# A two-layer graph attention kernel: the minimum of a merge's elu moved from VectorE to ScalarE, and new places for the steps of a hand-ordered schedule

## The chip, the cores and the metric

The kernel runs on one core of a Trainium2 chip. The metric is the time of one execution on the device in microseconds. A measurement of it is the median of several executions. A separate profiled execution gives the trace: every instruction with its engine, start and end. Its engines are called PE (TensorE's matmuls), PEld (its weight loads), DVE (VectorE), ACT (ScalarE), POOL (GpSimd) and SP (the queue that issues most DMAs).

## What is computed

Sixteen graphs of 1024 nodes with 256 features go through two layers. Layer 0 holds an MLP, an attention without a mask over all nodes ("dense"), a second MLP, and a masked attention; layer 1 is one more masked attention. Cut to what matters:

```python
h = relu(layernorm(x))                       # layer 0
out = relu(h @ mlp1_w + b1); residual = out  # 1024 x 512
out = gat(out, None, W_fc, a_fc)             # dense attention, ends in elu
out = elu(out) + residual                    # the merge: elu of an elu
out = relu(out @ mlp2_w + b2); residual = out
out = gat(out, adj, W_hand, a_hand)          # masked attention "a"
x = x + relu(elu(out) + residual)
h = relu(layernorm(x))                       # layer 1
x = x + relu(masked_gat(h, adj, W, a))       # masked attention "b"
```

with gat: h = inp @ W; e = leaky_relu(f1_i + f2_j); softmax over j; elu(att @ h). All of it is fp32.

## The kernel before

**Stages.** For each graph the dense attention needs no 1024 x 1024 matrix. Since leaky_relu has two branches, each node's mean over all others splits at a threshold into a sum over the nodes below it and a sum over those above. So the rows are ranked (`rank`, L911 ff.), scattered into sorted order in DRAM by GpSimd (`scatter`, L933), read back (`read_sorted`, L977), summed from both sides (`sum_before` L1005/L1007, `sum_behind` L1018/L1020), written as a fine table (L1012) with a coarse table of carried sums (`carry`, L1029 to L1034), and each node gathers its two rows (`gather`, L1044: first "fine", then "coarse" added onto it). `share` (L1056 to L1059) and `mean` (L1065, L1068) make the node's mean out of the gathered row. The first half of graph 0 takes matmuls instead (L1088, L1096). The projection ahead of it is a seven-product scheme for 2 x 2 blocks (`step`, L827, which adds to accumulators that ScalarE copies out in between, L849).

**The merge**, which the change edits, stands for one half h (512 nodes) and one chunk c (128 of 512 features): four transposes on TensorE into a PSUM tile (L1114), the minimum with 0 (L1116), exp (L1117), exp(. - 1) (L1118), which is the elu of the elu but for a constant folded into the later biases. `merge_end` adds max(ps, 0) on VectorE (L1124) and adds the sum to the residual on GpSimd (L1125). After four merges of a half, `mlp2` (L1132, evicted at L1135) reads it. The transposes' PSUM tile stays taken until `merge_end`; there are two such tiles ("tr"), four for matmul results ("mm"), and one double one ("bc").

**Masked attention** (Masked, Gnn0 for "a", Gnn1 for "b"): `project` (L662, L664), `extremes` (L669, L670), `vectors` (a transpose of the maxima at L539, then small VectorE and ScalarE steps, L679 to L691), `send` (a transpose at L544 and a DMA to DRAM) and `row` (a broadcast read back, L700), `scale` (L709), `weight` (L715, VectorE), `product` (L725, TensorE), and `finish`, `combine`, `add` and `update` (L737 to L771).

**Order.** The program is written step by step in the order of a table. `at(name, lo, hi, steps)` (L519 ff.) gives each step a time and adds a hand-set offset:

```python
when = lo + (hi - lo) * i / len(steps) + (moved[k] if k < len(moved) else 0.0)
table.append((when, len(table), step))
```

where `moved` is the entry of the dictionary SHIFT for the key part + name; part is "start ", "first ", "mid " or "end ". All steps are then sorted by `when` (L1532) and emitted; each engine carries out its instructions in that order, GpSimd too, whose order is tied by added dependences. The times have no effect but the order. The calls of `at` put the steps of graph b around base_of(b), with a period of 142 table units; steps of three graphs interleave: masked attention of b, dense attention of b+1, projection of b+2. Four of these calls:

```python
at("masked_first1", t0 + 1, t0 + 1, [m.vectors])
at("masked_first2", t0 + 3.4, t0 + 3.4, [m.send])
at("merges1", lo, lo + 9.2, each(d.merge, [h], range(HC)))
at("merges2", lo + 2.5, lo + 11.7, each(d.merge_end, [h], range(HC)))
```

Of the kernel before, what the change touches and what calls it, by code (L numbers as in the profile page):

```python
# [12 lines left out]
AF = mybir.ActivationFunctionType  # L13
# [18 lines left out]
    "end dense_begin1": (-4.8,),  # L32
    "end dense_begin2": (-4.19, -2.9,),
    "end dense_begin3": (-6,),
    "end dense_begin4": (0, -7.8, -7.7, -9.2, -13.5, -16, -18, -21.5,),
    "end dense_begin5": (-13, -8.9,),
    "end dense_begin6": (-15.56, -15.6, -23.8, -21.56, -18.8, -23.7,),
    "end dense_begin7": (-26.7,),
    "end dense_end1": (-11, -4.4,),
    "end dense_end2": (-10.8, -11.2, -9.8, -3.5, -3.4, 0, -3.1, -3.4,),  # L40
    "end dense_rows1": (-2.2, -2.09, -36.8, -18.9, -45.6, -25, -15.1, -10.1, 0, -24.9, -37.9,
        -13.5, -41.1, -31.4, -13.1, -24.8,),
    "end dense_rows2": (-13.8, -8, 0, 7, -11.8, -10, -21.5, -18.1, -13.6, -12, -13.5, 0, 4.5, 3.7,
        -16.8, -22.8, -10.4, -22.9, -9, -16.2,),
    "end dense_rows3": (0, -2.1,),
    "end dense_rows4": (-15.1,),
    "end dense_sums1": (-54.3,),
    "end dense_sums10": (-40.1,),
    "end dense_sums12": (-5.4,),
    "end dense_sums2": (0, -7.8, 7.9, 0, -6.2, -18.4, -20.7, -21.1,),  # L50
    "end dense_sums3": (-9.4, -4,),
    "end dense_sums4": (-9.7, -10.7, -8.6, -4.2, -4, -1.6, -2.3, -1.1,),
    "end dense_sums7": (-2.5, -3.7, -4.7, -4.3, -4.1, -4.8, -3.8, -4.43,),
    "end dense_sums9": (-2.3,),
    "end early_gathers1": (0, 0.002,),
    "end early_gathers2": (-6.42, -6.4,),
    "end early_gathers3": (12.5, 15.4, 9.3, 14,),
    "end early_gathers4": (0, -1.4, -3.64, 0, 8.4, 7.6, 3.7, 5.7,),
    "end first_mlp1": (-16.5, -17.2, -17.3, -3.7,),
    "end first_mlp2": (-54.3, -50.1, -81.4, -59.3,),  # L60
    "end masked_first1": (-15.6,),
    "end masked_first10": (-10.2, -10.6, -11.3, -10.4, -7, -7.4, -4.4, -5,),
    "end masked_first11": (-10.7, -11.3, -12.3, -9.9, -7.7, -7.4, -5.58, -6.198,),
    "end masked_first12": (-2.91,),
    "end masked_first13": (-12.5, -12.6, -12.6, -11.8,),
    "end masked_first14": (-9.41, -9.3, -12.4, -11.79, 2, 0.7, 0, -0.22,),
    "end masked_first15": (-11.7,),
    "end masked_first16": (-0.4,),
    "end masked_first2": (-15.1,),
    "end masked_first3": (-14.3,),  # L70
    "end masked_first4": (-13.9,),
    "end masked_first5": (-14.5, -14.5, -14.2, -10.7, -12.3, -13.74, -11.2, -12.8,),
    "end masked_first6": (-40.9,),
    "end masked_first7": (-24.2, 0, -18.5, -23.2,),
    "end masked_first8": (0, 0, 10.9, 2.8,),
    "end masked_first9": (-8, -8.5, -9.2, -9.1, -9.9, -8, -8.85, -9.6, -8.1, -7.8, -8.673, -9.54,
        -10.4, -11, -11.4, -11.3, -12.1, -12.7, -12.2, -11.3, -5.5, -4.5, -5.3, -6.16, -7.09, -4.2,
        -4.3, -3.7, -3.7, -4, -3.6, -3.9, -20.3, -12.1, -8.5, -7.3, -6.7, -6.9, -5.8, -5.1,),
    "end masked_second1": (-2.5, -3.1, -3.4, -3.71, -4.3, -4.9, -3.3, -3.3, -3.3, -3.3, -3.3, -3.3,
        -2.4, -2.4, -2.4, -2.4, -2.4, -2.4, -3.9, -2, -2.4, -2.8, 1.4, 1.4, 0, 0.9, 0.5, 0.7, 0.9,  # L80
        0.7, -24.9, -20.7, -20.7, -19.7, -14.1, -6.9,),
    "end masked_second2": (-5.2, -5.2, -1.8, -2.5, -2.1, -2.1, 2.1, 1.7, 0.3, -0.1, -10.9,),
    "end masked_second3": (-5.6, -5.7, -3.1, -2.3, -2.61, 1.2, 1.2, 0.002,),
    "end masked_second4": (-5.5, -3.8, 0, 3.4, -0.4, 0.5, 1.7, 15,),
    "end masked_second5": (40.4, 35, 28.4, 30.2, 28.1, 19.5,),
    "end masked_second6": (23.3, 19.2,),
    "end merges1": (-4.7, -6.7, -5.81, -8.1, 0, -2.6, 3.6, -1.7,),
    "end merges2": (-4.8, -6.5, -5.09, -7.39, 1.7, -0.62, 2.8,),
    "end scatters1": (0, -10.8, -13, -6.9, -16.54, -19.4, -20.05, -27.7,),
    "end second_mlp1": (-4.7, 1, -2.8, -3.8,),  # L90
    "end second_mlp2": (-22.5, -15.6, -13.3, -19.56, -20.4, -16.7, -19.3, -23.1,),
    "end second_mlp3": (-14.7,),
    "end second_norm1": (-6.7, -2.63, -6.7, -8.8, -5.2, -6.1, -7, -7.87,),
    "end second_norm2": (-8.5,),
    "end second_norm3": (-7.9,),
    "end second_norm4": (-8.6,),
    "end second_norm5": (-8.8, -8, -5.9, -8.1, -3.8, -4.4, -6.3, -6.3,),
    "end second_norm6": (-12.1,),
    "end second_norm7": (-14.9,),
    "end turn_at1": (-11.8, -11.8, -11.8, -11.8, -1.2, -1.6, -2, -2,),  # L100
    "end turn_at2": (-9.84, -9.8, -9.84, -9.8, -1.8, -1.8, -1.8, -1.8,),
    "end weights a": (-15.398, -15.1, -15.3, -15.8, -6.2, -14, -7.1, -18.2, -9.2, -11.5, -7.4,
        -18.7, -13.1, -9.4, -7.5, -9.2, -9, -12.2, -9, -8.3, -12.1, -8, -10.2, -14, -8.8, -7.3,
        -8.2, -5.93, -8, -5.9, -6.6, -5.4, -15.5, -12.8, -12.7, -13.6, -15.3, -8.1, -7.7, -7,),
    "end weights b": (-8.4, -8.8, -8.2, -8.6, -9.7, -6.8, -4.6, -2, -7.6, -4.6, -7, -4.6, -1.8,
        -3.2, -1.4, -1.9, -4.9, -5.7, -8.6, -2.4, -5.6, 0, 0, 0, 0, 0, 0, -1.3, 0, 0, -8.8, 0,
        -1.6, 3.34, 0, 0, 0, 2.1, 2.5, 1.5, -22.7, -21.8, -23.1, -42.3, -15.4, -19.8, -11.1,
        -11.9,),
    "first dense_begin1": (-2.9,),
    "first dense_begin2": (0, 0.002,),  # L110
    "first dense_begin3": (-3.39,),
    "first dense_begin4": (3.7, 1.7, 0, -2.6, -4.5, -8.8, -14.1, -13.2,),
    "first dense_begin5": (-6.2, -6.2,),
    "first dense_begin6": (-19, -21, -26.9, -36.497, -21.9, -18.1,),
    "first dense_end1": (-7.5,),
    "first dense_end2": (-6.1, -5, -3.64, -5.2, 8.6, 4.9, 9.2, 3.9,),
    "first dense_rows1": (-16.9, -16.5, -16.7, -16.797, -15.6, -15.6, -17.9, 3.8, 0, 2.5, -29.3,
        -25, -23.9, -19.68, -8.7, -20.8,),
    "first dense_rows2": (-20.8, -20.6, -17.1, -14.6, -18.7, -13.1, -13.4, -12.6, -12.9, -15.1,
        -11.7, 2.03, 0, 3.2, -20.3, -17.5, -10.4, -19.3, -8.4, -7.1,),  # L120
    "first dense_rows3": (-6.5, -1.9,),
    "first dense_rows4": (-11.5,),
    "first first_mlp1": (-7.1, 0, 0, 17.6,),
    "first first_mlp2": (-6.2, -4, -22.9, -6.4,),
    "first first_norm3": (-32.1, -26.6, -29.2, -30, -31.1, -29.4, -21.9, -22.7,),
    "first first_norm4": (-24.9,),
    "first first_norm5": (-36.6, -36.6, -36.6, -36.6, -28, -47.3, -48.1, -27.4,),
    "first first_norm6": (-33.7, -33.7, -33.7, -33.7, -32.7, -34.1, -27.5, -33.4,),
    "first first_norm7": (0, 0.003, 0.003, 0.003,),
    "first gathers1": (4.6, 4.6, 4.6, 4.6, -5.6, 0, 11.4, 11.5,),  # L130
    "first gathers2": (12.8, 13.4, 10.5, 9.9, -9.8, 0, 0, -1.2,),
    "first masked_first1": (-8.2,),
    "first masked_first10": (-6.3, -6.7, -7.6, -7.9, -2.21, -2.3, -4.9, -5.46,),
    "first masked_first11": (-5.8, -7.2, -3.8, -4.6, -2, -2.2, -4.6, -5.19,),
    "first masked_first13": (-9.1, -4.5, -4.7, -8.3, -4.9, -5.6, -7.9, -8.5,),
    "first masked_first14": (-5.1, 0, -3.1, -3.9, -3.2, -4.7, -7.84, -8.44,),
    "first masked_first15": (-6.1,),
    "first masked_first16": (-8.9,),
    "first masked_first4": (-10.2,),
    "first masked_first5": (-7.4, -7.4, -7.4, -7.4, -7.4, -7.4, -7.4, -7.4,),  # L140
    "first masked_first6": (-185.7,),
    "first masked_first8": (4.4, 14.6, 16.2,),
    "first masked_first9": (-5.9, -6.7, -7.1, -7.7, -8.4, -6.6, -7.4, -7.5, -11.7, -9.7, -10.5,
        -9.8, -10, -10.2, -10.6, -8.5, -2.6, -2.6, -2.6, -2.6, -2.6, -2.6, -2.6, -2.6, -4.6, -4.6,
        -4.6, -4.6, -4.6, -4.6, -4.6, -4.6,),
    "first masked_second1": (-31.7, -26.8, -20.2, -18.5, -14.3, -13.7, -4.9, -3.5, -3.7, -2.7, 0,
        0, -6.2, -5.8, -5.2, 0, 0, 0, -1.6, -1.6, -1.6, -1.6, -1.6, -1.6,),
    "first masked_second2": (-13.8, -13.8, 0, 0, 0.8, 0.8, -1.8, -1.8,),
# [164 lines left out]
def fast_path(ctx: ExitStack, tc: tile.TileContext, alarm, x, adj, w1, b1, w2, b2, w_fc, a_fc,  # L313
# [21 lines left out]
    nc = tc.nc  # L335
# [441 lines left out]
    class Dense:  # L777
# [331 lines left out]
        def merge(self, h, c):  # L1109

            ps = tr_psum(f"hpT_{self.b}_{h}_{c}")
# [350 lines left out]
    e = dense[1]  # L1462
# [528 lines left out]
```

## Time and profile before

| what | us |
|---|---|
| median of 3 runs | 2241.82 (2232.39 to 2243.66) |
| the profiled execution | 2232.1 |
| its span, first to last instruction | 2230.4 |
| TensorE busy in it | 2172.5 |
| VectorE, ScalarE, GpSimd busy | 1776.0, 1261.9, 1067.5 |
| granted TensorE clock, mean | 0.997 |

A row of the groups reads: line, engine, operation, out<-in, shapes, count, then the busy time in us and the mean ns of one, then the engine's idle time just before these instructions and what ended it. A row of the waits reads: the waiting engine and line, who ended the wait, the sum in us, how many, the longest. In a row of the timeline the bracket holds the idle time ahead of the instruction and its releaser.

### The profile page before, as it was taken

The numbers are of one execution on the slowest core, as the hardware profiler recorded it, in microseconds if no ns is written. First come the engines' busy times: TensorE is split into PE (matmuls) and PEld (weight loads), VectorE is DVE, ScalarE is ACT, GpSimd is POOL, SyncE is SP. The second block draws the span as 40 slices with busy tenths as digits, with TensorE's granted clock in tenths as the row PEclk, the third lists the DMA queues.
The fourth block names the chain that finished last, engine by engine and source line by source line (L and its number), as shares of the span: only waits on it lengthen the run. The fifth ranks groups of instructions, "written<-read, shape, count | busy, mean of one in ns | idle before, by whom it ended". The sixth has DMA issues, their size and how long they took to land. (4 is left out here: it accounts for less than half of the span.)

```text
span 2230.4 us, 31158 instructions
## 1 busy us (share of the span) xinstructions
PE 2172.5 (97%) x9498; PEld 1672.8 (75%) x9498; DVE 1776.0 (80%) x4929; ACT 1261.9 (57%) x2797; POOL 1067.5 (48%) x1344
## 2 busy tenths in 40 slices
PE   7989999999999999999999999999999999999998
PEld 4757778687876878778687877868788687777777
DVE  7877887788877779887888878778887878869756
ACT  5446655647465573756547465563755657455453
POOL 3343527365362744627375363735537265463520
PEclk9999999999999999999999999999999999999999
DMA  6367758566576756757666575856748574565610
GB/s 226 115 166 202 152 181 189 176 172 173 165 178 191 180 159 187 181 161 173 202 170 166 174 177 178 189 176 178 175 150 202 187 177 136 167 172 161 162 41 28
DMA packets 268751, 373.42 MB, mean 167 GB/s; under 512 B 124880, under 2 KB 180760, under 8 KB 264480
## 3 DMA queue, kind: packets, MB, share of 16 engines
q1 hardware_dynamic: 221968, 207.19, 32.6%
q0 software_dynamic: 45952, 163.99, 28.9%
q8 instruction: 78, 1.28, 0.3%
q14 instruction: 97, 0.79, 0.1%
q10 hardware_dynamic: 656, 0.17, 0.0%
HBM read 231.09 MB, written 126.56 MB: 160 GB/s over the span
## 5 line engine op out<-in xcount | busy, mean ns | idle before, releaser
L725 PE MATMUL ob<-hmb,attb 128*128 128x257 f32 x2048 | 473.3, 381 | 0.4 <-DVE attb L715 0.2
L725 PE MATMUL oa<-hma,atta 128*128 128x258 f32 x2048 | 459.8, 382 | 6.0 <-ACT resT L801 4.4
L725 PEld LDWEIGHTS oa<-hma,atta 128*128 128x128 f32 x2048 | 385.8, 190 | 74.0 <-ACT resT L801 9.2
L725 PEld LDWEIGHTS ob<-hmb,attb 128*128 128x128 f32 x2048 | 382.0, 191 | 57.5 <-issue 5.4
L715 DVE SCALAR_TENSOR_TENSOR atta<-rowsa,qwda,edge 128x256 f32<-128x256 f32 (+1 forms) x520 | 239.8, 494 | 71.8 <-DMA rowsa<-row_a 67.6
L753 POOL TENSOR_TENSOR posa<-posa,onat 128x256 f32<-128x256 f32 x118 | 98.5, 835 | 384.3 <-ACT posa L741 383.6
L715 DVE SCALAR_TENSOR_TENSOR attb<-rowsb,qwdb,edge 128x256 f32<-128x256 f32 (+1 forms) x536 | 268.0, 528 | 8.2 <-PE ob L725 4.1
L1044 POOL DMA_INDIRECT got<-coarse,k x124 | 202.8, 1635 | 96.6 <-DMA got<-fine,k 38.4
L798 PE MATMUL m<-hT,w_sb 128*128 128x512 f32 x512 | 238.4, 596 | 0.3 <-ACT hT L588 0.2
L1132 PE MATMUL m<-resT,w_sb 128*128 128x512 f32 x512 | 229.3, 599 | 8.7 <-POOL resT L1125 8.5
L1125 POOL TENSOR_TENSOR resT<-resT,e 128x512 f32<-128x512 f32 x128 | 167.5, 1320 | 110.6 <-DVE e L1124 103.5
L933 POOL DMA_INDIRECT sorted<-hnat,place x128 | 126.8, 991 | 143.0 <-DVE place L926 53.5
L740 ACT ACTIVATE ea<-oa,reca 128x256 f32<-128x256 f32 x128 | 60.7, 474 | 236.2 <-DVE reca L737 214.1
L1132 PEld LDWEIGHTS m<-resT,w_sb 128*128 128x128 f32 x512 | 95.6, 192 | 118.4 <-issue 99.0
L801 ACT ACTIVATE resT<-m,b_sb 128x512 f32<-128x512 f32 x128 | 87.4, 685 | 159.8 <-PE m L798 159.8
L1044 POOL DMA_INDIRECT got<-fine,k x124 | 130.3, 1051 | 64.7 <-DMA fine<-xs 26.3
L798 PEld LDWEIGHTS m<-hT,w_sb 128*128 128x128 f32 x512 | 96.1, 191 | 80.1 <-issue 73.2
L956 ACT ACTIVATE junk<-r,fs 128x1024 int8<-128x1024 f32 x124 | 142.1, 1146 | 11.1 <-POOL fs L860 6.5
L754 POOL TENSOR_TENSOR ea<-ea,posa 128x256 f32<-128x256 f32 x118 | 99.1, 839 | 90.4 <-ACT ea L747 59.5
L767 ACT ACTIVATE rb<-ob,recb 128x256 f32<-128x256 f32 x128 | 57.9, 474 | 146.0 <-DVE recb L765 136.2
L1068 DVE SCALAR_TENSOR_TENSOR hp<-got,den,part 128x513 f32<-128x513 f32 x120 | 103.9, 878 | 38.6 <-ACT part L1065 36.9
L1117 ACT ACTIVATE e<-e 128x512 f32<-128x512 f32 x128 | 79.9, 624 | 95.7 <-DVE e L1116 94.5
(211 smaller groups left out, 4314.0 us busy)
## 6 DMA issues: line engine op xcount, KB each, us to landing
xs<-sorted SPq DMA_DIRECT2D x32, 1028.0 KB
fine<-tt SPq DMA_DIRECT2D x32, 1026.0 KB
fine<-xs SPq DMA_DIRECT2D x32, 1026.0 KB
x<-in_x_dram SPq DMA_DIRECT2D x16, 1024.0 KB
xn<-in_x_dram SPq DMA_DIRECT2D x15, 1024.0 KB
out_dram<-x SPq DMA_DIRECT2D x28, 512.0 KB
hT<-xn SPq DMA_DIRECT2D x416, 32.0 KB
coarse<-carry SPq DMA_DIRECT2D x32, 256.5 KB
```

What stands on the lines that cost most here:

```text
L715: nc.vector.scalar_tensor_tensor(a_t[:, :n * P], self.rows[:, i], self.qwd[:, 1, j:j + 1], edge[:, j, i], op0=OP.max, op1=OP.mult)
L725: nc.tensor.matmul(self.out[t][:, :F + self.ONES], lhsT=self.att[t0, j][:, (t - t0) * P:(t - t0 + 1) * P], rhs=self.hm[:, j, 2:2 + F + sel ...
L753: adder.tensor_add(pos, pos, o_nat[:, t, :])
L754: adder.tensor_add(e, e, pos)
L798: nc.tensor.matmul(ps, lhsT=w1_sb[:, kc, c * P:(c + 1) * P], rhs=piece(kc, h), start=(kc == 0), stop=(kc == FC - 1))
L801: nc.scalar.activation(self.resT[:, c, h * HALF:(h + 1) * HALF], ps, AF.Relu, bias=b1_sb[:, c:c + 1])
L933: made = nc.gpsimd.indirect_dma_start(out=sorted_d[self.b % 2], out_offset=bass.IndirectOffsetOnAxis(ap=self.place[:, t:t + 1], axis=0), i ...
L956: nc.scalar.activation(junk, self.r2, AF.Sign, bias=self.fs[:, 0, t:t + 1], accum_out=self.signs[:, t:t + 1])
L1044: nc.gpsimd.indirect_dma_start(out=got[u // n][:, u % n, :], out_offset=None, in_=(coarse_d if coarse else fine_d)[self.b % 2][:, :], in_o ...
L1068: nc.vector.scalar_tensor_tensor(hp, got[:, K:], den[:, 0, u:u + 1], part, op0=OP.mult, op1=OP.add)
L1125: nc.gpsimd.tensor_add(dst, dst, e)
L1132: nc.tensor.matmul(ps, lhsT=w2_sb[:, kc, c * P:(c + 1) * P], rhs=self.resT[:, kc, h * HALF:(h + 1) * HALF], start=(kc == 0), stop=(kc == H ...
```

## The change

In `merge` the minimum with 0 leaves VectorE: ScalarE computes relu(-mean) from PSUM, and the first exp takes the scale -1. exp(-relu(-m)) is exp(min(m, 0)), so the result is the same. Beside that nearly all entries of SHIFT get new values, so that nearly every step of the program may stand at another place of the order. The steps themselves are the same 7005 in both.

```diff
             e = work.tile([P, HALF], F32, tag="e2", name=f"e_{self.b}_{h}_{c}", bufs=3)
-            nc.vector.tensor_scalar_min(e, ps, 0.0)
-            nc.scalar.activation(e, e, AF.Exp)
+            nc.scalar.activation(e, ps, AF.Relu, scale=-1.0)
+            nc.scalar.activation(e, e, AF.Exp, scale=-1.0)
             nc.scalar.activation(e, e, AF.Exp, bias=neg1)
```

Of SHIFT, the entries that bear on the steps named below (the diff has some 270 lines more of this kind):

```diff
-    "end early_gathers4": (0, -1.4, -3.64, 0, 8.4, 7.6, 3.7, 5.7,),
+    "end early_gathers4": (-8.55, -6.9, -1.7, -3.7, 9.2, 11.4, 4.7, 4.7,),
...
-    "end dense_end1": (-11, -4.4,),
+    "end dense_end1": (-12.1, -3.3,),
...
-    "mid dense_sums3": (-4.26,),
+    "mid dense_sums3": (-0.158609, -2.5,),
...
-    "mid masked_first1": (-9.2,),
+    "mid masked_first1": (-13.3,),
...
-    "mid masked_first2": (-9.61,),
+    "mid masked_first2": (-12.2,),
...
-    "mid merges1": (1.1, 0, 3.22, 0.92, 7.4, 10.3, 8.1, 5.8,),
-    "mid merges2": (3.6, 1.4, 3.4, 0.5, 5.5, 7.83, 10.4, 9.1,),
+    "mid merges1": (2.75, -2.3, 5, 3.5, 6.8, 4.5, 7.2, 6.6,),
+    "mid merges2": (6.3, 0, 4.5, 2.4, 4.5, 4.1, 7.5, 5.6,),
...
-    "mid second_norm8": (0, -20.95, -9.6, -17.3, -21.9, -14.21, -21.2, -13,),
-    "mid second_norm9": (-4.6,),
+    "mid second_norm8": (-18.9, -20.8, -18.8, -26, -24.9, -25.4, -25.5,),
+    "mid second_norm9": (-16.7,),
...
-    "start merges1": (-14.1, -15.5, -17, -15.4, 0, 5.5, 5, -11.3,),
-    "start merges2": (-16.4, -14.7, -9.8, -9.53, 3.55, 5.6, 3.9, -3.5,),
+    "start merges1": (-20.6, -21.8, -22.6, -24.5, 0, 2.7, 0.43, -10.4,),
+    "start merges2": (-16.4, -16.5, -17.6, -19.4, 7.8, 5.5, 4.8,),
```

In the order that follows, the steps of the middle repeat from period to period, before and after.

## The prediction

> **What bounds the kernel now.** I read the page's head first, then TensorE's share by stretches of the span, then who ended TensorE's waits, and only then the rows of the instructions that the change touches.
>
> ```profile
> span 2230.4 us, 31158 instructions
> ...
> PE 2172.5 (97%) x9498; PEld 1672.8 (75%) x9498; DVE 1776.0 (80%) x4929; ACT 1261.9 (57%) x2797; POOL 1067.5 (48%) x1344
> ```
>
> ```profile
> 0.00:200.00 200.00, 172.27 (x747) 121.25 (x748) 157.58 (x466) 93.85 (x182) 68.56 (x110) 0.97 0.59 174
> 200.00:1960.00 1760.00, 1746.06 (x7593) 1348.09 (x7593) 1426.24 (x3920) 1030.29 (x2308) 902.14 (x1121) 1.00 0.66 175
> 1960.00:2230.40 270.40, 254.14 (x1160) 203.49 (x1159) 192.19 (x543) 137.77 (x309) 96.82 (x114) 0.99 0.40 110
> ```
>
> The columns of the second view are the stretch, its length, then the busy time of PE, PEld, DVE, ACT and POOL, TensorE's granted clock, the DMA share and GB/s. TensorE (PE) is the bound. It is idle 27.7 us in the first 200 us, 13.9 us in the middle 1760 us, and 16.3 us in the last 270 us. The change leaves every matmul as it is, so no more than these 57.9 us (2.6%), and what a stall costs inside the "busy" time, can be won. The waits:
>
> ```profile
> PE m L1132 <- POOL resT L1125: 8.5, 3, 3.9
> ...
> PE oa L725 <- ACT resT L801: 4.4, 7, 1.3
> PE extpsb L539 <- DVE extb L670: 4.0, 2, 3.6
> PE linea_ps L544 <- ACT qwda L687: 3.5, 10, 0.4
> ```
>
> 8.5 us lie in the start (three waits of mlp2 for the merged rows of graph 0), 4.0 in the end, 3.5 are ten waits of one kind, one per period of the middle. The rest are scattered waits of a few tenths, and 10 us before the first transpose.
>
> **The elu's minimum.** Durations from the rows (busy, then mean ns):
>
> ```profile
> L1118 ACT ACTIVATE e<-e,neg 128x512 f32<-128x512 f32 x128 | 92.4, 722 | 4.2
> ...
> L1116 DVE TENSOR_SCALAR e<-hpT 128x512 f32<-128x512 f32 x128 | 84.8, 680 | 10.7 <-PE hpT L1114 10.2 <-issue 0.2
> L1117 ACT ACTIVATE e<-e 128x512 f32<-128x512 f32 x128 | 79.9, 624 | 95.7 <-DVE e L1116 94.5
> ...
> L588 ACT ACTIVATE hT<-nt 128x512 f32<-128x512 f32 x76 | 41.0, 592 | 72.1 <-PE nt L584 72.0
> ```
>
> Removed: 128 VectorE minima by 0.680 us, 87 us of 1776. Added: 128 ScalarE Relus from PSUM. The trace has no such Relu with scale -1, but L588 is a Relu of the same shape from PSUM without a pointer operand: 0.592 us; L801, with a bias pointer, takes 0.685. I take 0.592, 76 us, ScalarE then at 60%; the other end is 88 us. The Exp with scale -1 costs what it cost. Table loads: none, since Relu (L740) and Exp (L746) alternate already and the trace has one table load of 1283 ns in all.
>
> A rule of the Trainium skill speaks against this step: "ScalarE: Activation LUTs", section "Rules for kernel authors", wants relu, max and min on VectorE, which it calls up to about 3x faster per element in bf16. By the rule the minimum would be 0.592/3 = 0.2 us on VectorE, and the change would give up 25 us there for 76 us on ScalarE. By the rows VectorE needs 0.680 on this fp32 PSUM source and ScalarE 0.592, so 87 us are freed for 76. The rows decide. The chain of one merge becomes 0.592+0.624+0.722 = 1.94 us instead of 2.03, but all of it on ScalarE, whose own part was 1.35. So merges that come back to back now leave at one per 1.94 us.
>
> In the middle the merges are not back to back. In table order, counting TensorE's own work between steps (0.217 us per matmul record of 257 columns, 0.109 per transpose, 0.43 per 512 columns), the first half's four merges of a period are spread over 10.1 us instead of 5.6, the second half's over 6.7 instead of 7.6. Between the last merge of the first half and the mlp2 that reads it there are 8.2 us instead of 11.4. Needed: 1.94+0.69 (L1124)+1.32 (L1125) = 3.95 us plus ScalarE's lag. That covers a lag of 4 us. If the cover is gone, TensorE stands for the excess in each period; this is the second rival below. Likeliest: nothing.
>
> **The new places, middle.** The ten waits of the row transpose (L544):
>
> ```profile
> 960.31 0.27 PE L539 MATMUL extpsa<-ident,exta 128*128 128x128 f32 x1
> 960.42 1.03 PE L725 MATMUL ob<-hmb,attb 128*128 128x257 f32 x4
> 961.80 0.27 PE L544 MATMUL linea_ps<-ident,qwda 128*8 128x128 f32 x1 [0.35 <-ACT qwda L687]
> ```
>
> From the transpose of the maxima to the row transpose the chain VectorE, then Exp on ScalarE takes 1.49 us, and one product step (0.87) lies between. The table puts the two at 1.0-9.2 = -8.2 and 3.4-9.61 = -6.21 before, and at -12.3 and -8.8 after; in the new order two product steps (1.74 us) lie between. 1.74 + 0.11 exceeds 1.49, so this wait goes: -3.5 us. What is late next there is the product's wait for mlp1's eviction (L725 <- L801, 4.4 us): its TensorE order (mlp1 c=3, natural 1 and 2, then ga product) is the same after, so 0. VectorE and ScalarE steps are moved throughout; VectorE's 87 us less can only help its queue, ScalarE's 76 more can hurt evictions; bounds -8 to +27 (second rival), taken 0.
>
> **The end.** The longest single wait:
>
> ```profile
> 2092.14 0.45 PE L539 MATMUL extpsb<-ident,extb 128*128 128x128 f32 x1 [3.62 <-DVE extb L670]
> 2092.38 3.46 PE L725 MATMUL ob<-hmb,attb 128*128 128x257 f32 x8
> ```
>
> Eight matmuls in 3.46 us are 0.43 each, twice the usual 0.217: the stretch from 2092 to 2096 shows a granted clock of 0.57, so 1.7 of these 4.0 us are lost too. The chain of work that ended last tells the cause: VectorE stood 6.38 us at the share (L1056) of graph 15's first half until its last coarse gather, issued at 2080.77, landed 10.02 us later, and extb (L669, L670) is queued behind it. "end early_gathers4" moves the first two of these gathers by -8.55 and -6.9: the last is issued 8.9 us of TensorE work ahead of the share instead of 5.2. 3.7 us more cover removes the 3.6 us: -3.6-1.7 = -5.3. On GpSimd's queue the last two coarse gathers (1.64 each) and one fine gather (1.05) now stand ahead of the second root of graph 14's norm (L569, L570: 0.52+1.09), which VectorE's centering just before the share waits for. That is 3.3+1.05+1.6 = 6.0 us of queue from 8.7 us of TensorE work away: covered by 2.7 us; with the cover gone, the excess is TensorE's again, as its turns and the share come behind the centering. I take 0 for it, and -2 to -5.3 for the whole.
>
> **The start.** Before, merge (0,0) begins at 134.58 and the fourth quarter of the first mlp2 at 153.17, with half the clock from 148 to 154. After, TensorE's work ahead of merge (0,0) grows from 111.9 to 116.2 us (dense products and one step are drawn ahead), so it begins near 138.9, and the four merges are paced by ScalarE: 0.4+4x1.94+0.69+1.32 = 10.2, so 149.1. That is 4 us earlier than 153.17. But GpSimd, in order, has coarse gathers of 1.6 us between the adds, and the second half hangs on the landing of its last gather as before. I take -2, between -6 and +8 (back to back merges that end later than reckoned, at half clock).
>
> **Landings.** The profiled execution took 2232.1, its span 2230.4; the median of the three runs is 2241.8, 9.7 above. I take the difference to be landings that came later and what waits for them; no trace here shows a slower execution. The new order gives the sorted rows 9.5 us of TensorE work from read to first use instead of 3.9, and the row of the second layer 10.4 instead of 6.5. It takes back between 0 and 9.7; for want of a row I take 3.
>
> Sum: -3.5-5.3-2-3 = -13.8, from 2241.8 to 2228.0 us, or 2221 for an execution like the profiled one.
>
> **The rivals.** (1) More is won: the new places also clear the scattered waits. The middle's other 10 us, half of the start's 17.8 us beside the first 9.9, and the 9.7 of landings instead of 3 would make another 20: 2208. For it: VectorE is at 80% and waits 67.6 us for row reads. Against: these waits are many and of 0.2 to 0.8 us, each with its own cause. (2) Slower: ScalarE is late in the merges. Its load there now:
>
> ```profile
> 901.40:909.70 8.30, 8.30 (x40) 7.23 (x39) 5.84 (x19) 8.09 (x20) 4.22 (x4) 1.00 0.97 199
> 909.70:918.00 8.30, 8.30 (x45) 7.20 (x44) 6.77 (x17) 6.94 (x18) 7.03 (x8) 1.00 1.00 167
> 918.00:926.20 8.20, 8.20 (x43) 7.11 (x42) 6.58 (x14) 6.83 (x17) 4.86 (x5) 1.00 0.30 61
> ```
>
> The fourth busy column sums to 21.9 of 24.8 us. Eight Relus add 4.7: 26.6, 1.8 too many. ScalarE also evicts the seven-product's accumulators (L849), which TensorE adds to again a few steps later, and mm has four banks; so a lag of over about 4 us is TensorE's wait. 1.8 us in each of 15 batches are 27: 2269. It decides if less than 1.8 us of other ScalarE work leaves this stretch. In the new order four of eight scale steps (L709, 4x0.5 = 2.0 us) leave, but two sign steps (1.3 each) come in at its end. (3) The stalls only move: what is cleared at one place returns at the next queue, 2241.
>
> **How the numbers follow.** Likeliest case 0.42 at 2228 (by itself 2218 to 2238), more won 0.18, stalls move 0.19, slower 0.21. Within 0.5% of 2241.8 is 2230.6 to 2253.0; half a per cent is about what a measurement of this kernel can tell from no change. Of the likeliest case two thirds lie under 2230.6: faster 0.28+0.18 = 0.46; same 0.14+0.19 = 0.33; slower 0.21. The range goes from 2206 to 2258: from the case of more won to the lower part of the slower one.
>
> **What would show it.** Right: no waits of linea_ps on qwda; TensorE's gap before extpsb near the end under 1 us with full clock after it; DVE busy near 1690, ACT near 1338, the new Relu near 0.59; the middle's TensorE idle time near 10 us. Wrong: new waits of TensorE on ScalarE's L849, L664 or L801 between merges, or on L1125, of over 1 us per period; or a start whose mlp2 begins later than 150.

## The result, and the profile after

| | before | after |
|---|---|---|
| median, us (four runs each) | 2240.64 (2232.39 to 2243.66) | 2210.82 (2207.67 to 2213.08) |
| profiled execution / its span | 2232.1 / 2230.4 | 2209.0 / 2207.3 |
| ratio after/before, 95% interval | | 0.9872 [0.9841, 0.9902] |

The change makes the kernel faster by 29.8 us between the medians and by 23.1 us between the two profiled spans. The forecast had the sign, and its range (2206 to 2258) holds the time; but its likeliest case was 2228, and the time is near the first rival's 2208. So more was won than its steps account for.

The head of the page after, with the busy time of each engine:

```profile
PE 2162.5 (98%) x9498; PEld 1678.0 (76%) x9498; DVE 1689.1 (77%) x4801; ACT 1336.2 (61%) x2925; POOL 1064.5 (48%) x1344
```

VectorE (DVE) lost 128 instructions and 86.9 us, ScalarE (ACT) got 128 and 74.3 us. The number of matmuls is the same. The three stretches of the span after, with the columns of the prediction's second view (the third is shorter because the kernel ends earlier):

```profile
0.00:200.00 200.00, 174.72 (x748) 126.12 (x749) 156.43 (x457) 100.44 (x193) 69.87 (x110) 0.95 0.61 177
200.00:1960.00 1760.00, 1755.41 (x7695) 1367.56 (x7694) 1358.05 (x3846) 1104.54 (x2447) 913.05 (x1134) 1.00 0.67 178
1960.00:2207.00 247.00, 232.38 (x1058) 184.29 (x1056) 174.60 (x500) 131.25 (x286) 81.61 (x101) 0.99 0.36 103
```

The count in the second row is the first thing to see: in the same 1760 us TensorE gets through 7695 matmul records instead of 7593. It is idle 4.6 us there instead of 13.9. TensorE's waits over the whole span after, the first four rows (who ended the wait; sum, number, longest, in us):

```profile
PE nt L591 <- DVE hn L581: 11.5, 2, 9.9
PE hpT L1121 <- DVE e L1131: 7.6, 5, 4.1
PE hpT L1121 <- issue: 2.3, 2, 1.9
PE m L805 <- ACT rb L774: 2.2, 6, 0.5
```

(Line numbers after are those of before plus 7.) The first row is the start, where the first transpose waits 9.9 us in both kernels. Of the four rows shown in the prediction, three have left the list: the row transpose's ten waits for qwda, the product's seven for mlp1's eviction, and mlp2's three for the merged rows of graph 0. The last has its successor in the second and third rows, also in the start. The end's wait for extb is 1.5 instead of 4.0.

**Where the time came from.** Idle time alone falls by 13.1 us (57.9 to 44.8), the busy time of TensorE by 10.0. The busy time of the same matmuls can fall because a short wait can lie inside what a record counts as busy: the row transpose's waits of before are 3.5 us of idle time, but 5.6 us from start to start. I therefore added up, from the trace, how much later each matmul record starts than the usual pitch after the one before it (0.217 us for 257 columns, 0.429 for 512, 0.109 for a transpose). These sums hold both kinds of stall, and what matmuls lose at a lower clock; they leave out the time before the first matmul and after the last:

| stalls of TensorE, us | start, to 180 | middle, 180 to 1975 | end |
|---|---|---|---|
| before | 29.2 | 31.2 | 16.6 |
| after | 30.5 | 9.4 | 14.0 |
| difference (sum -23.1) | +1.3 | -21.8 | -2.6 |

The gain is in the middle. From one graph's first mlp2 to the next graph's a period takes 131.2 us instead of 133.0, on the mean of the eleven from the third graph to the fourteenth: 20.0 us in all, nearly the same by another way. In before's 31.2 the largest parts are the product's wait for mlp1's eviction (6.3, start to start), the row transpose's for qwda (5.6), the transposes of the merges (3.4), and the seven-product's for hmb (3.0) and hnat (2.1). All of them are near 0 after. New after is one of 3.2, mlp1's wait for ScalarE's rb (L805 <- L774; 2.2 of it idle, in the fourth row above).

### The profile page after: what moved, and what is told of

It reads as the page before. It is cut to its first block, busy times and chain, and to the rows that moved or that the text cites. A ratio compares the mean times of both kernels' runs of the same rounds, so it can differ in the third digit from the quotient of the medians.

```text
span 2207.3 us, 31327 instructions
## 1 busy us (share of the span) xinstructions
PE 2162.5 (98%) x9498; PEld 1678.0 (76%) x9498; DVE 1689.1 (77%) x4801; ACT 1336.2 (61%) x2925; POOL 1064.5 (48%) x1344
## 4 chain that ended last, share of the span: by engine, by line
PE 85%; DVE 6%; POOL 5%; ACT 2%; issue 1%; DMA 0%; POOLq 0%; DVEq 0%; ACTq 0%
PE oa L732 19%; PE h L834 17%; PE ob L732 13%; PE m L805 10%; PE m L1139 9%; PE pb L669 5%; PE pa L669 5%; POOL got L1051 3%; PE hpT L1121 3%; PE nt L591 1%; PE on L1153 1%; DVE attb L722 1%; PE od L1103 1%; PE carry L1036 1%; POOL ea L761 1%
## 5 line engine op out<-in xcount | busy, mean ns | idle before, releaser
L732 PE MATMUL ob<-hmb,attb 128*128 128x257 f32 x2048 | 465.5, 381 | 1.9 <-DVE attb L722 1.1
L722 DVE SCALAR_TENSOR_TENSOR atta<-rowsa,qwda,edge 128x256 f32<-128x256 f32 (+1 forms) x520 | 265.7, 542 | 61.9 <-DMA rowsa<-row_a 48.8
L722 DVE SCALAR_TENSOR_TENSOR attb<-rowsb,qwdb,edge 128x256 f32<-128x256 f32 (+1 forms) x536 | 238.7, 480 | 17.6 <-PE ob L732 8.0
L805 PE MATMUL m<-hT,w_sb 128*128 128x512 f32 x512 | 237.8, 597 | 2.7 <-ACT rb L774 2.2
L774 ACT ACTIVATE rb<-ob,recb 128x256 f32<-128x256 f32 x128 | 58.0, 473 | 242.5 <-DVE recb L772 236.3
L805 PEld LDWEIGHTS m<-hT,w_sb 128*128 128x128 f32 x512 | 95.7, 191 | 88.9 <-issue 73.0
L1051 POOL DMA_INDIRECT got<-fine,k x124 | 134.8, 1087 | 57.6 <-issue 29.0
L963 ACT ACTIVATE junk<-r,fs 128x1024 int8<-128x1024 f32 x124 | 142.4, 1148 | 9.0 <-issue 3.8
L1131 DVE SCALAR_TENSOR_TENSOR e<-hpT,e 128x512 f32<-128x512 f32 x128 | 87.7, 686 | 68.1 <-ACT e L1125 50.5
L808 ACT ACTIVATE resT<-m,b_sb 128x512 f32<-128x512 f32 x128 | 87.7, 687 | 85.0 <-PE m L805 84.4
L834 PE MATMUL h<-wfc_sb,resT 128*128 128x257 f32 x512 | 129.3, 383 | 0.3 <-ACT hpd L1113 0.3
```

Source lines behind the costliest of these rows:

```text
L722: nc.vector.scalar_tensor_tensor(a_t[:, :n * P], self.rows[:, i], self.qwd[:, 1, j:j + 1], edge[:, j, i], op0=OP.max, op1=OP.mult)
L732: nc.tensor.matmul(self.out[t][:, :F + self.ONES], lhsT=self.att[t0, j][:, (t - t0) * P:(t - t0 + 1) * P], rhs=self.hm[:, j, 2:2 + F + sel ...
L805: nc.tensor.matmul(ps, lhsT=w1_sb[:, kc, c * P:(c + 1) * P], rhs=piece(kc, h), start=(kc == 0), stop=(kc == FC - 1))
L834: nc.tensor.matmul(ps, lhsT=lhs[:, k, :], rhs=rhs[k], start=start and k == 0, stop=k == 1, skip_group_check=True)
L963: nc.scalar.activation(junk, self.r2, AF.Sign, bias=self.fs[:, 0, t:t + 1], accum_out=self.signs[:, t:t + 1])
L1051: nc.gpsimd.indirect_dma_start(out=got[u // n][:, u % n, :], out_offset=None, in_=(coarse_d if coarse else fine_d)[self.b % 2][:, :], in_o ...
```

## The experiments

Three theories stand in the expectations. V: the gain comes from VectorE's relief. P: it comes from the new places, above all of the steps that wait for landings. S: the new places spread the merges, so that ScalarE's longer part in each no longer holds TensorE up. The prediction's own second rival (ScalarE late in the merges) is tested by the same runs. All ratios are to the kernel before; the times of its further runs have medians of 2235.5 to 2238.2. No experiment leaves out a part of the computation.

**1. The minimum alone.** The kernel before, with the two edited lines of the merge and every old place:

```diff
-            nc.vector.tensor_scalar_min(e, ps, 0.0)
-            nc.scalar.activation(e, e, AF.Exp)
+            nc.scalar.activation(e, ps, AF.Relu, scale=-1.0)
+            nc.scalar.activation(e, e, AF.Exp, scale=-1.0)
```

> The kernel before with ScalarE's Relu and the Exp of scale -1 in the merge, all steps at their old places. Theory P (the gain is the new places, above all where ScalarE's queue waits for landings): no gain by this alone, 2236 to 2250 us against 2241 before, and a little slower if ScalarE is late in the merges; the eviction wait of the masked product (L725 on L801) and the row transpose's wait (L544) stay. Theory V (VectorE's 87 us less is what TensorE gains from): 2225 us or less, with VectorE busy 1690 and few of these waits.

Measured: 2265.06 us (2264.35 to 2279.09), ratio 1.0143 [1.0113, 1.0174]. TensorE's waits from 200 to 1960 us:

```profile
PE hpT L1114 <- DVE e L1124: 14.9, 24, 1.0
PE h L827 <- ACT hnat L849: 7.8, 13, 0.6
```

The transposes of a merge need a PSUM tile, which is free only when `merge_end` (L1124, VectorE) has read it, and `merge_end` needs exp(. - 1) from ScalarE (L1118 before). In this stretch VectorE waits 72.8 us for that exp here, 21.2 in the kernel before and 39.1 in the kernel after. 24 waits are two per period. The second row is the copy of the seven-product's accumulators, queued on the same engine. The middle's stalls are 56.2 us instead of 31.2. So VectorE's 87 us less are worth nothing by themselves. ScalarE late in the merges, the second rival, is real: 32.8 us between the profiled spans, where it was priced at 27. Most of it comes by the merge's own tiles (18.8 us from start to start), less by the copies of accumulators that the rival named (10.9).

**2. The places alone.** The kernel after, with the minimum back on VectorE. (With the minimum there, the new start places of the merges put minima ahead of the `merge_end` that frees their tiles on VectorE's queue, so the start's merges have their old places here.)

```diff
-    "start merges1": (-20.6, -21.8, -22.6, -24.5, 0, 2.7, 0.43, -10.4,),
-    "start merges2": (-16.4, -16.5, -17.6, -19.4, 7.8, 5.5, 4.8,),
+    "start merges1": (-14.1, -15.5, -17, -15.4, 0, 5.5, 5, -11.3,),
+    "start merges2": (-16.4, -14.7, -9.8, -9.53, 3.55, 5.6, 3.9, -3.5,),
...
-            nc.scalar.activation(e, ps, AF.Relu, scale=-1.0)
-            nc.scalar.activation(e, e, AF.Exp, scale=-1.0)
+            nc.vector.tensor_scalar_min(e, ps, 0.0)
+            nc.scalar.activation(e, e, AF.Exp)
```

> The kernel after with the minimum back on VectorE; only graph 0's merge and merge_end steps in the start stand at their old places, as the new ones put minima ahead of the merge_end steps that free their PSUM tiles. Theory P: most of the gain stays, 2211 to 2222 us, TensorE's idle time between 200 and 1960 us stays near 5 us. Theory V: the gain is mostly gone, 2230 to 2245 us, with new waits of TensorE on VectorE.

Measured: 2278.32 us (2275.19 to 2278.56), ratio 1.0181 [1.0158, 1.0205]. The waits from 200 to 1960 us:

```profile
PE h L834 <- DVE hnat L866: 21.7, 12, 1.8
PE line_ps L551 <- DVE fs L887: 13.5, 12, 1.1
```

Twelve waits each, one per period, and all on VectorE. The places alone cost more than the minimum alone, and only the two together gain: theory P as a whole falls. The new order needs a VectorE that is relieved, the old one a ScalarE that is not loaded.

**3. Old places of the middle.** The kernel after, with all entries of the middle as before (two of them shown):

```diff
-    "mid masked_first2": (-12.2,),
+    "mid masked_first2": (-9.61,),
...
-    "mid merges1": (2.75, -2.3, 5, 3.5, 6.8, 4.5, 7.2, 6.6,),
+    "mid merges1": (1.1, 0, 3.22, 0.92, 7.4, 10.3, 8.1, 5.8,),
```

> The kernel after with the middle's entries of before (start, first and end new, ScalarE's minimum kept). By the traces the middle is worth 20 of the 23 us between the profiled executions, so 2231 to 2240 us; if the middle's old places are worse with the merges wholly on ScalarE, 2240 to 2255 us. Rival (the gain is in start and end): 2215 to 2222 us.

Measured: 2267.92 us (2261.32 to 2271.55), ratio 1.0120 [1.0093, 1.0148]; the middle's stalls are 70.1 us, and the longest of its waits are those of experiment 1 again (the line numbers here are those of before plus 5):

```profile
PE hpT L1119 <- DVE e L1129: 15.7, 24, 1.0
PE h L832 <- ACT hnat L854: 8.5, 15, 0.6
```

The gain lies in the places of the middle. The new start and end do not bring it.

**4. The merges close together again, in the new order.** The kernel after, with the first half's four merges of a period at their old places:

```diff
-    "mid merges1": (2.75, -2.3, 5, 3.5, 6.8, 4.5, 7.2, 6.6,),
-    "mid merges2": (6.3, 0, 4.5, 2.4, 4.5, 4.1, 7.5, 5.6,),
+    "mid merges1": (1.1, 0, 3.22, 0.92, 6.8, 4.5, 7.2, 6.6,),
+    "mid merges2": (3.6, 1.4, 3.4, 0.5, 4.5, 4.1, 7.5, 5.6,),
```

> The kernel after with the first half's merges in the middle back at their old places, two pairs back to back (within 0.9 us of TensorE work each) where the new places have 3 and 2 us between. Theory S: waits of transposes on merge ends (L1131) come back, 0.7 to 1.5 us per period, 2220 to 2230 us. Rival: 2209 to 2214 us.

Measured: 2259.95 us (2252.48 to 2261.6), ratio 1.0102 [1.0080, 1.0123]; 43.1 us more span than the kernel after. The waits from 200 to 1960 us:

```profile
PE h L834 <- ACT hnat L856: 26.1, 24, 1.4
PE h L834 <- DVE hnat L866: 10.5, 12, 0.9
```

These are not the waits expected at the merge's own tile. Four merges need 4 x 1.94 = 7.8 us of ScalarE and stand within 5.7 us of TensorE's work, and the accumulators' copies (L856) queued among them come too late, twice per period. One such place, from ScalarE's and TensorE's timelines:

```profile
925.25 0.72 ACT L1125 ACTIVATE e<-e,neg 128x512 f32<-128x512 f32 x1
925.88 0.63 ACT L856 COPY hnat<-h 128x257 f32<-128x257 f32 x2
...
926.28 2.00 PE L834 MATMUL h<-wfc_sb,s 128*128 128x257 f32 x8 [1.40 <-ACT hnat L856]
```

The middle's stalls go from 9.4 to 55.7 us. Within the new order theory S holds, at another line and larger than expected.

**5. The spread merges in the old order.** Experiment 1 with only the new middle entries of the merges:

```diff
-    "mid merges1": (1.1, 0, 3.22, 0.92, 7.4, 10.3, 8.1, 5.8,),
-    "mid merges2": (3.6, 1.4, 3.4, 0.5, 5.5, 7.83, 10.4, 9.1,),
+    "mid merges1": (2.75, -2.3, 5, 3.5, 6.8, 4.5, 7.2, 6.6,),
+    "mid merges2": (6.3, 0, 4.5, 2.4, 4.5, 4.1, 7.5, 5.6,),
```

> The first experiment (old places, minimum on ScalarE) with the middle's merges and merge ends at their new places. Theory S (ScalarE's pace of 1.94 us per merge against two PSUM tiles makes the cost, and spreading the merges takes it off): the transposes' waits on L1124, 18.8 us of TensorE's stalls in the middle, fall to under 7, 2265 to 2248-2254 us; the 11 us of waits on L849 stay. Rival (total ScalarE load): waits only change their line, 2260 us or more.

Measured: 2376.14 us (2370.91 to 2382.23), ratio 1.0621 [1.0593, 1.0649]. The waits from 200 to 1960 us:

```profile
PE h L827 <- ACT lineb L546: 23.9, 12, 2.1
PE m L1132 <- POOL resT L1125: 21.6, 11, 2.0
PE hpT L1114 <- DVE hp L1068: 19.9, 20, 1.7
PE h L827 <- ACT hnat L849: 17.2, 17, 1.4
```

The third row tells one reason: the first two merges of the second half now stand right behind the last of its means (L1068), which were not moved. By the table, counted from the base of their graph, these two merges stand at 105.0 (105.6 and 110.8 in experiment 1) and the last two means at 103.6 and 103.9; the kernel after has the means at 94.3 to 95.4. What S expected of this kernel failed.

**6. The means moved too.** Experiment 5, with the new places of the middle's dense rows as well (two entries of six shown):

```diff
-    "mid dense_rows3": (-2.4, -2.1,),
-    "mid dense_rows4": (-7.3,),
+    "mid dense_rows3": (-1.7, -6.7,),
+    "mid dense_rows4": (-19.6,),
```

> The same with the middle's steps of the seven-product (sums, steps, pair adds, load of b21) at their new places too. Theory S: the accumulators' waits on L849 fall as well since more TensorE work stands between two steps of one accumulator, 2236 to 2246 us. Rival: no better than with the merges alone.

Measured: 2337.61 us (2335.87 to 2339.73), ratio 1.0451 [1.0426, 1.0476]. The waits for L849 fell as expected, but 17.8 us of mlp2's waits for resT and 15.8 of the transposes' for L1068 remain, and others came. A part of the new order in the old one is worse than either order.

**7. The sums behind the eviction.** The prediction put the product's wait for mlp1's eviction (L801) at 0 change. At 1105.12 us in the kernel before, ScalarE's timeline and TensorE's are:

```profile
1104.00 0.30 ACT L996 ACTIVATE bd<-xs,topd 128x4 f32<-128x4 f32 x1 [1.57 <-DMA xs<-sorted]
...
1104.40 0.67 ACT L801 ACTIVATE resT<-m,b_sb 128x512 f32<-128x512 f32 x1
...
1105.12 5.05 PE L725 MATMUL oa<-hma,atta 128*128 128x258 f32 x22 [0.52 <-ACT resT L801]
```

The eviction waits for nothing of its own. It is queued behind L996, the sums' weights of the next graph, and that waits 1.57 us for the sorted rows to land. The product pays 0.52 us for it. After, the two stand the other way round, and there is no wait:

```profile
1092.93 0.69 ACT L808 ACTIVATE resT<-m,b_sb 128x512 f32<-128x512 f32 x1
1093.52 0.29 ACT L1003 ACTIVATE bd<-xs,topd 128x4 f32<-128x4 f32 x1
```

The edit makes that exchange alone in the kernel before:

```diff
-    "mid dense_sums3": (-4.26,),
-    "mid dense_sums4": (-5.2, -5.2, -5.2, -5.2, 0.28, -0.96, -2.208, -3.2,),
+    "mid dense_sums3": (-2.4,),
+    "mid dense_sums4": (-3.38, -4.62, -5.2, -5.2, 0.28, -0.96, -2.208, -3.2,),
```

> The kernel before with one thing moved in the middle: the first half's sums_weights (ScalarE waits there for the sorted rows) goes from just ahead of mlp1's fourth eviction to just behind it, and the first two sum_before steps follow it; their order on VectorE stays. Theory P: the waits of the masked product on mlp1's eviction (4.4 us in 7 waits, about 6.3 us with the restart) vanish: 2232 to 2237 us. Rival (ScalarE's lag is its load, or the wait moves to the next eviction): 2239 to 2243 us, the waits stay or come back on L1148 or L996's successors.

Measured: 2238.14 us (2231.27 to 2242.61, 12 runs), ratio 1.0004 [0.9987, 1.0021]. The wait for L801 went from 6.3 us of stalls to near 0, and ScalarE's waits for sorted rows from 26.6 to 11.8 (in the middle from 1.0 to 2.4 us a period to nearly none); yet the middle's stalls are 32.5 instead of 31.2. The product then waits for its weights (atta, 2.1) and for others without one name (3.2). The diagnosis was right and worth nothing alone: the rival that a cleared stall returns at the next queue holds here.

**8. The sums early, in the new order.** The kernel after, with the sums' weights ahead of the evictions again.

```diff
-    "mid dense_sums3": (-0.158609, -2.5,),
+    "mid dense_sums3": (-4.26, -2.5,),
```

> The kernel after with the same step undone: in the middle the first half's sums_weights goes 4.1 table units earlier, so that it stands 3.5 us of TensorE work behind the read (9.5 in the kernel after, 3.9 in the one before) and ahead of mlp1's third and fourth evictions. Theory P: ScalarE waits for the landing with evictions queued behind it, TensorE's waits on L808 come back, 0.7 to 1.5 us in each of some 12 periods: 2220 to 2230 us, and executions spread wider. Rival: the other new places cover it, 2209 to 2214 us.

Measured: 2261.64 us (2256.09 to 2265.92), ratio 1.0112 [1.0087, 1.0136]; 49.6 us more span than the kernel after. TensorE's longest sum of waits is now:

```profile
PE on L1153 <- ACT onat L1155: 33.1, 22, 3.5
```

and one such place, in ScalarE's timeline and TensorE's, is:

```profile
1116.92 0.30 ACT L1003 ACTIVATE bd<-xs,topd 128x4 f32<-128x4 f32 x1 [5.39 <-DMA xs<-sorted]
...
1118.29 0.67 ACT L1155 ACTIVATE onat<-on,neg 128x512 f32<-128x512 f32 x1
...
1119.01 0.66 PE L1153 MATMUL on<-ident,oT 128*128 128x128 f32 x4 [2.25 <-ACT onat L1155]
```

ScalarE stands for 5.39 us before one instruction of 0.30, with evictions behind it. Its waits for sorted rows are 77.1 us instead of 17.7. Part of the loss is TensorE's clock: behind the wait shown, from 1120 to 1123 us, it was granted at 0.50, and over the run at 0.989 instead of 0.994. So P holds for this place, at L1155 more than at the expected L808. It is not experiment 7 turned round, though: ScalarE waits here 4.3 to 6.6 us in nearly every period, where the kernel before waited 1.0 to 2.4. So 49.6 us is what this early place costs in the new order, and not what the change won by leaving the old one.

**9. More work ahead of the row transpose.** The reason that the prediction gave for -3.5 us, tested alone in the kernel before: a second product step between the transpose of the maxima and the row transpose.

```diff
-    "mid masked_first2": (-9.61,),
+    "mid masked_first2": (-8.1,),
```

> The kernel before with one thing moved in the middle: the send of the first layer's row goes 1.5 table units later, so that two product steps (1.74 us) instead of one stand between the transpose of the maxima and the row transpose. The prediction's step: the ten to twelve waits of L544 vanish, -3.5 us and up to -5.6 with the restart of the weight loads: 2235 to 2238 us. Rival: the row lands later by the same time, VectorE's weights come later and TensorE waits for them instead: 2241 us or more.

Measured: 2253.63 us (2250.44 to 2258.09), ratio 1.0067 [1.0042, 1.0093]: slower. The row transpose's waits are gone, and the first of the waits is:

```profile
PE oa L725 <- ACT resT L801: 20.1, 11, 2.5
```

`send` does not only transpose: its DMA is followed on SP's queue by the row's read, which waits for the send's landing, and the read of the sorted rows is queued behind that. Medians counted from the transpose of the maxima, before and here: the row transpose at 1.49 and 1.84 us, the row's read issued at 3.42 and 4.56, the sorted read at 4.05 and 5.19, the first use of the sorted rows at 10.9 and 11.8. So ScalarE waits 43.0 us for sorted rows instead of 26.6, with mlp1's eviction behind it. The kernel after avoids this: by TensorE's own work ahead of them, its transpose of the maxima stands about 1.8 us earlier in each period than before, so that the row transpose still comes about 0.9 us earlier, and the sums' weights stand behind the eviction.

**10. The end's gathers alone.** The kernel before with

```diff
-    "end early_gathers4": (0, -1.4, -3.64, 0, 8.4, 7.6, 3.7, 5.7,),
+    "end early_gathers4": (-8.55, -6.9, -1.7, -3.7, 9.2, 11.4, 4.7, 4.7,),
```

> The kernel before with one entry of the new places: the first-half coarse gathers of the last two graphs earlier (the entry of end early_gathers4). The prediction's step: the 3.62 us gap of TensorE before the last-but-one extpsb goes and the half clock behind it: -5.3 us, 2236 us. Rival: the gathers land no earlier, since they come behind their fine gathers on GpSimd's queue, and the share waits as before: 2241 us.

Measured: 2236.28 us (2231.74 to 2239.52, 12 runs), ratio 0.9991 [0.9976, 1.0006]; too little to tell from no change by the times. In the trace the waits for extb are 2.1 us instead of 4.0, and the end's stalls 14.5 instead of 16.6: -2.1, not -5.3.

**11. The start's merges.** The kernel after, with the old start places of the merges:

```diff
-    "start merges1": (-20.6, -21.8, -22.6, -24.5, 0, 2.7, 0.43, -10.4,),
-    "start merges2": (-16.4, -16.5, -17.6, -19.4, 7.8, 5.5, 4.8,),
+    "start merges1": (-14.1, -15.5, -17, -15.4, 0, 5.5, 5, -11.3,),
+    "start merges2": (-16.4, -14.7, -9.8, -9.53, 3.55, 5.6, 3.9, -3.5,),
```

> The kernel after with graph 0's merges and merge ends in the start at their old places. The prediction's step gave the start's new places 2 us, between -6 and +8: 2211 to 2215 us. The traces so far show the start's stalls alike before and after (29 and 30 us), so by them no difference, 2208 to 2213 us; above 2216 us if the new places are what keeps the start from being worse with ScalarE's slower pace.

Measured: 2216.04 us (2213.26 to 2224.13), ratio 0.9912 [0.9889, 0.9936]. The start's stalls are 36.9 us; in the kernel after they are 30.5, and before, with the minimum on VectorE, 29.2. The new start places give back what the minimum on ScalarE costs there at the old ones, and no more. At the old places three of ScalarE's rank steps (L963) hold it from 138.84 to 142.52 us, while the first merge's transposes, begun at 139.30, wait for its Relu.

No version tried is faster than the kernel after.

## Why the prediction was right, and where not

| step | predicted | measured (stalls, or as said) |
|---|---|---|
| row transpose's wait | -3.5 | gone: -5.6 |
| product's wait for mlp1's eviction | 0 | -6.3 |
| the rest of the middle | 0 | -9.9 |
| the end | -5.3 | -2.6 |
| the start | -2 | +1.3 |
| landings (median less profiled execution) | -3 | -6.7 in four runs each, less with more |
| sum | -13.8 | -29.8 |

**The elu's minimum: right.** The row of the new Relu, by its shape (busy, mean ns, then the idle time before it and what ended it):

```profile
L1123 ACT ACTIVATE e<-hpT 128x512 f32<-128x512 f32 x128 | 75.5, 590 | 42.3 <-PE hpT L1121 33.5 <-PE extdps L546 4.8 <-POOL hnat L868 2.7
```

590 ns, where 592 was taken from the nearest row; VectorE 1689 and ScalarE 1336 us, where 1690 and 1338 were forecast. ScalarE waits for TensorE before it, not the other way round: in this order it is not late. The 0.2 us that the prediction set against it for VectorE came from a figure for bf16, and these rows are fp32, so nothing here tests that figure.

**The middle: the step that failed.** "What is late next there is the product's wait for mlp1's eviction ... its TensorE order ... is the same after, so 0." The order on TensorE was the wrong one to compare. The eviction is ScalarE's, and what made it late was the DMA wait ahead of it on ScalarE's queue, which the change moves behind it. Experiments 7 and 8 show that. They also show that it can't be priced by itself: moving the step behind the eviction was worth 0 in the old order, and moving it ahead again, to a still earlier place, costs 49.6 us of span in the new one.

The second half of the failure is in the first rival's argument against itself: "these waits are many and of 0.2 to 0.8 us, each with its own cause". Of before's 31.2 us in the middle, four waits on ScalarE (for mlp1's eviction, qwda, hmb and hnat) make 17.0, and all four are near 0 after. Experiments 4 and 8 speak against "its own" too: each moves one kind of step, 4 merges of 8 or one step of sums, and either brings more stalls (46.3 and 51.0 us) than the 21.8 that all the new places of the middle took away. That points to a common cause, what stands ahead of these on ScalarE's queue; a run shows it for mlp1's eviction (experiment 7), not for each of the others.

**The first rival: near in number, partly by luck.** Its 2208 lies close to 2210.8, but its sum does not come out: 10 + 8.9 + 6.7 are 25.6 us beyond the likeliest case (23.6 if the 2 us already taken for the start are left out), not 20. And the start, counted in at 8.9, gave nothing. The middle gave the 10 and more, and VectorE's waits for row reads, which spoke for it, fell from 67.6 to 48.8 us. Of the signs named, the middle's idle time was to be near 10 us and is 4.6.

**The row transpose: right number, incomplete reason.** The wait went, as reckoned. But more work between the two transposes, the reason given, costs more than it gains when done by moving `send` (experiment 9). The prediction missed SP's queue there. In the kernel after there are two product steps between the transposes, and the second transpose has no bracket:

```profile
1081.26 0.27 PE L546 MATMUL extpsa<-ident,exta 128*128 128x128 f32 x1
1081.37 1.90 PE L732 MATMUL ob<-hmb,attb 128*128 128x257 f32 x8
1083.11 0.27 PE L551 MATMUL linea_ps<-ident,qwda 128*8 128x128 f32 x1
```

**The end: right in kind, half the size.** The long wait is 0.76 us instead of 3.62, and the clock stays at 1.00:

```profile
2069.29 0.29 PE L546 MATMUL extpsb<-ident,extb 128*128 128x128 f32 x1 [0.76 <-DVE extb L677]
2069.42 1.03 PE L732 MATMUL ob<-hmb,attb 128*128 128x257 f32 x4
```

Four matmuls take 1.03 us there, where eight took 3.46. At this place alone 2.9 + 1.7 = 4.6 us are won; the end as a whole has 2.6. The other 2.0 came back in small stalls, from start to start: the product's for attb (0.4 before, 1.4 after), the merges' transposes for `merge_end` (0 and 0.8), the projection's for mlp2's eviction (0.9 and 1.4). What set each of them off was not traced. The share still waits 3.84 us for its coarse gather (6.38 before), so the gather gained 2.5 us of cover, not the 3.7 reckoned. The risk that the prediction put at 0 did come, on VectorE alone: the centering (L581) waits 3.04 us for the root that stands behind the gathers on GpSimd's queue (0.87 before). So the 2.7 us of cover counted for it were not there, and TensorE had other work meanwhile.

**The start: half right.** Merge (0,0) begins at 138.8 us, where 138.9 was reckoned, and mlp2's 8.5 us of waits are gone. Their successors were not reckoned: 6.9 us of the next transposes for the tile that `merge_end` still holds, and 2.3 that wait for nothing the profile shows. The longest of these, 4.12 us, is not ScalarE's pace of 1.94 us per merge: ScalarE was through with the second merge at 142.71 us, but VectorE had rank steps (L926 to L933, one of 2.51 us) ahead of its `merge_end` until 145.60. That queue was not in the reckoning. And TensorE's granted clock over the first 200 us is 0.95 instead of 0.97.

**The second rival** was right about the engine and nearly about the size, for another order than the one that it was meant for. It holds when the merges are close together (experiments 1, 3 and 4), and the new places spread them. But spreading alone is no cure (experiment 5).

**Landings.** Between median and profiled execution lie 8.5 us before and 1.8 after in the first four runs of each. Over 11 to 17 later runs of the kernel before it is 3.4 to 6.1. So the term is -1.6 to -4.3, and the -3 was a guess that came out well. Measured against the medians of those later runs (2235.5 to 2238.2) the whole gain is 25 to 27 us and not 29.8. What differs from one execution to the next no trace here shows.

**Open.** How the 21.8 us divide among the many new places can't be told: single moves do not add up, in either order. Of the middle's -9.9 only the waits' names are known.

## What to carry to other kernels

When an operation goes to another engine, the order of the whole program may have to follow: here the move alone cost 1.4%, the new order alone 1.8%, and together they gave 1.3%. For a wait of TensorE on an eviction, read what stands ahead of that eviction on its own engine's queue: if it waits for a DMA, TensorE waits for the DMA, and the cure is to exchange the two, with a look at what is late next. And for each step that is moved, follow all the instructions that it issues, DMA queues too, before its gain is booked.

## What was not expected of the hardware

- A matmul of a stalled TensorE may look busy: of the 23.1 us won in the span, 10.0 were in "busy" time of the same 9498 matmul records, and a lower clock is only a part of them (1.7 us at the end's long wait). Starts of records showed these, the waits did not.
- Where ScalarE already waits for the sorted rows, the time from the issue of their read to their first use is nearly the same: in the median 6.8 us before, 6.7 in experiment 9 and 6.8 in experiment 8. So a later issue is paid by the reader: with the issue 1.1 us later (experiment 9), its median wait grew from 1.4 to 2.8 us.
- One instruction of 0.30 us on ScalarE, put too early, cost 49.6 us of span (experiment 8): it blocks its queue for up to 6.6 us at a time, and TensorE's clock falls behind some of these waits.
